# Softmax weights of a windowed attention, already with keys on the partitions: transposed after the softmax, or computed so from second scores

## The chip, the cores and the metric

One core of a Trainium2 chip runs the whole program in one launch. The metric is device time in microseconds, median of several runs. All data are float32.

## What is computed

A gated cross-attention block, then a gated mixture of expert biases, on x of shape (8, 512, 2048): 8 batches, 512 features D, 2048 positions S. Only the attention is touched by the change.

```python
x = x + tanh(g_xattn[0]) * xattn(layernorm(x, axis=-1), ctx, masks, Wq, bq, Wk, bk, Wv, bv, Wo, bo)
x = x + tanh(g_ffn[0]) * ffn(layernorm(x, axis=-1), router_weight, router_bias, expert_bias)

def xattn(qk, v, masks, ...):          # DK = 256, H = 8 heads of dh = 32, windows of W = 128 positions
    qp, vp, mp = patches of 128 positions of qk, v, masks
    q = Wq @ qp + bq;  k = Wk @ qp + bk;  val = Wv @ vp + bv
    scores = einsum('bhdi,bhdj->bhij', qh, kh) / sqrt(dh)
    scores = where(mp[:, :, None, :] > 0, scores, -1e9)
    attn = softmax(scores, axis=-1)
    o = gelu(einsum('bhij,bhdj->bhdi', attn, vh))
    return (Wo @ o + bo) * masks
```

Each window of 128 positions attends only to itself, so for each window and head the scores are a 128 x 128 square (queries i, keys j). The second product contracts over the keys, and TensorE contracts over the partitions of its operands: it wants the weights with the keys on the partitions, while the softmax's row sums and maxima are taken along the free axis, with the queries on the partitions.

## The kernel before, in words

The 128 windows are handled in 64 **groups** g of two windows (NPP = 2, 256 positions); two groups make a **chunk** of 512 positions (32 chunks, four per batch). Groups with even g are the first half of a chunk, odd ones the second. The order of instructions on every engine is written out by hand (`manual_schedule`), and every engine works through its own list in order. One iteration of the main loop (line 816, 62 groups; the last two groups are written out behind it) does parts of several groups in a software pipeline:

- scores of group g (`scores`, line 412): 16 products into four PSUM banks sc0 to sc3, one bank for each of four heads that lie on 32 partitions each; each product of float32 shows as two records on TensorE;
- the weighed values of group g-2 (`weigh`, 487), and their copy to SBUF by ScalarE (`weighed`, 504, the copy is at line 480);
- row maxima (`maxima`, 431, VectorE): 16 instructions that write min(-(score + mask bias)) per row as a column `nmx`, and the negated masked scores as `at`;
- exponentials (`exps`, 446, ScalarE), in place, with row sums;
- in the old way, the division by the sums (`divide`, 458: reciprocal on VectorE, product on GpSimd), and for group g-1 four *turns*: `turn` (468) transposes four heads on TensorE, `turned` (482) copies the result to SBUF on ScalarE;
- queries and keys of the next chunk, one half of the features per group (`queries_and_keys`, 343: seven blocks of products by a Strassen-like scheme, with VectorE and GpSimd adding between them; `between` is called in it at set places);
- values of the next chunk (`values`, 391, and `values_out`, 402, which adds the bias bv on VectorE);
- even groups: layer norm of a later chunk (`norm`, 264, ScalarE), half of the output projection (`attend`, 524, two of four), and four transposes of the result for the router (`turn_x`, 549); odd groups: GELU with its table load, `table_of_exps` (212, which loads the table of the exponential back), the router's `logits` (557), and the other half of `attend`;
- at the end of each group one step of the expert mix of an earlier batch (`mix`, 749): two products pb, and two additions on VectorE that read them.

A PSUM bank that is written again must first be read out. The projections and the mix share a pool of two banks (`ps_mm`, tag mm), transposes and weighed values another of two (`ps_tr`, tag tr); from the third group on, the values of a group go into bank sc0 (`values(c_, h_, 0, 0)`), and half of `attend` in odd groups into sc1 and sc2 once the mix runs. Loads and stores are issued on SP's queue, except for the first context and x tiles, and one last store, on ScalarE's.

Of the kernel before, what the change touches and what calls it, by code (L numbers as in the profile page):

```python
# [22 lines left out]
def flamingo_gated_kernel(  # L23
# [51 lines left out]
    ps_mm = ctx.enter_context(tc.tile_pool(name="ps_mm", bufs=2, space=PSUM))  # L75
    ctx.enter_context(tc.manual_schedule())
# [46 lines left out]
    bv_sb = const.tile([P, DK], F32, name="bv_sb")  # L123
# [4 lines left out]
    gates = const.tile([P, 2], F32, name="gates")  # L128

# [24 lines left out]
    def load_rest():  # L154
# [3 lines left out]
        nc.sync.dma_start(bv_sb, bv.partition_broadcast(P))  # L158
        with nc.allow_non_contiguous_dma(reason="short bias vectors onto partitions"):
            nc.sync.dma_start(bq_sb, bq.rearrange("(t p) -> p t", p=P))  # L160
            nc.sync.dma_start(bk_sb, bk.rearrange("(t p) -> p t", p=P))
            nc.sync.dma_start(bo_sb, bo.rearrange("(t p) -> p t", p=P))
        nc.sync.dma_start(gates[:, 0:1], g_xattn.partition_broadcast(P))
# [4 lines left out]
    def load_later_weights():  # L168
        nc.sync.dma_start(wo_sb, woT.rearrange("(t p) d -> p t d", p=P))
        nc.sync.dma_start(rw_sb, rwT.rearrange("(k p) e -> p k e", p=P))  # L170

# [171 lines left out]
    def queries_and_keys(ch, e, between):  # L343
# [6 lines left out]
        s1, s5, u2, u4 = (  # L350
            work.tile([P, CW // 2], F32, tag=t, name=f"{t}_{ch}_{e}", bufs=1)
            for t in ("s1", "s5", "u2", "u4")
        )
# [14 lines left out]
        nc.vector.tensor_tensor(u2, p6, s1, ALU.add)  # L368
        banks.append(product([P, 2, CW // 2], f"qk_{ch}_{e}_1"))
# [5 lines left out]
        between(0)  # L375
# [3 lines left out]
        u3 = work.tile([P, CW // 2], F32, tag="s1", name=f"u3_{ch}_{e}", bufs=1)  # L379
# [3 lines left out]
        between(1)  # L383
# [3 lines left out]
        nc.vector.tensor_tensor(k, k, m01s[ch], ALU.mult)  # L387
# [14 lines left out]
    def values_out(ch, h):  # L402
# [3 lines left out]
        nc.vector.tensor_tensor(vT, pv, bv_sb[:, None, :].to_broadcast([P, NPP, DK]), ALU.add)  # L406
# [3 lines left out]
    pairs = {}  # L410

    def scores(g):


        ch, h = g // NH, g % NH
        sc = [ps_sc.tile([P, NPP, NE, W], F32, tag=f"sc{r}", name=f"sc_{g}_{r}") for r in range(HR)]
        rows = [slice(r * DH, (r + 1) * DH) for r in range(HR)]
        for i in range(NPP):
            ws = slice(h * HW + i * W, h * HW + (i + 1) * W)
            for e in range(NE):  # L420
                for r in range(HR):
                    nc.tensor.matmul(  # L422
                        sc[r][:, i, e, :], qss[ch][rows[r], e, ws], kss[ch][rows[r], e, ws],
                        start=True, stop=True,
                    )
        nmx = small.tile([P, HR, NPP, NE], F32, tag="nmx", name=f"nmx_{g}")
        at = [work.tile([P, H, W], F32, tag="at", name=f"at_{g}_{i}", bufs=4) for i in range(NPP)]
        rsum = small.tile([P, NPP, H], F32, tag="rsum", name=f"rsum_{g}")
        pairs[g] = {"sc": sc, "nmx": nmx, "at": at, "rsum": rsum, "atT": {}}

    def maxima(g, qs):
# [4 lines left out]
        for q in qs:  # L436
            i = q // 2
            bias = m01s[ch][:, hf * HW + i * W : hf * HW + (i + 1) * W]
            for r in (2 * (q % 2), 2 * (q % 2) + 1):
                for e in range(NE):  # L440
                    nc.vector.tensor_tensor_reduce(  # L441
                        p["at"][i][:, e * HR + r, :], p["sc"][r][:, i, e, :], bias, -1.0, BIG,
                        ALU.add, ALU.min, p["nmx"][:, r, i, e : e + 1],
                    )

    def exps(g, q):
        p = pairs[g]
        i = q // 2
        for r in (2 * (q % 2), 2 * (q % 2) + 1):
            for e in range(NE):  # L450
                h = e * HR + r
                at = p["at"][i][:, h, :]
                nc.scalar.activation(  # L453
                    at, at, AF.Exp, bias=p["nmx"][:, r, i, e : e + 1], scale=-1.0,
                    accum_out=p["rsum"][:, i, h : h + 1],
                )

    def divide(g, i, engine=None):
        p = pairs[g]
        rs = p["rsum"][:, i, :]  # L460
        nc.vector.reciprocal(rs, rs)  # L461
        (engine or nc.gpsimd).tensor_tensor(  # L462
            p["at"][i], p["at"][i], rs[:, :, None].to_broadcast([P, H, W]), ALU.mult
        )

    os_ = {}

    def turn(g, k):
# [3 lines left out]
        if e == 0:  # L472
            p["atT"][i] = work.tile([P, H, W], F32, tag="atT", name=f"atT_{g}_{i}")
# [5 lines left out]
    def copy(engine, out_, in_):  # L479
# [748 lines left out]
```

## Time and profile before

| | us |
|---|---|
| device time, median of 3 runs | 1311.58 |
| lowest and highest run | 1311.1, 1311.7 |
| span of the profiled execution | 1309.1 |
| busy: TensorE, VectorE, ScalarE, GpSimd | 1292.1, 923.7, 872.2, 796.3 |
| L476 the turns on TensorE, 1024 x 275 ns | 150.7 (they overlap) |
| L480 their copies on ScalarE, 254 x 576 ns | 140.5 |
| L422 scores on TensorE, 2048 records x 283 ns | 75.6 (they overlap) |
| L462 divisions on GpSimd, 128 x 1908 ns | 244.2 |
| DMA: 173.40 MB, mean 132 GB/s | 40% of 16 engines on SP's queue |

The profile is one execution recorded by the hardware. A line such as `618.34 1.17 PE L422 MATMUL sc<-ks,qs ... x32` in its timeline is a merged group: start and length in us, engine, source line, operation, what is written from what is read, shapes, and how many records. PE is TensorE's products, PEld its weight loads, DVE is VectorE, ACT ScalarE, POOL GpSimd; SPq and ACTq are the instructions on SP's and ScalarE's sequencers that issue DMAs. Records of one engine overlap a little, so cost is read from start to start. A bracket at a line's end is the idle time before it and what ended it.

### The profile page before, as it was taken

The page shows a single profiled execution, that of the slowest core. Times are in us where ns is not written, and L with a number is a line of the kernel's source. Part 1 is how long each engine was busy: PE and PEld are TensorE (multiplying, and loading weights), DVE is VectorE, ACT ScalarE, POOL GpSimd, SP SyncE. Part 2 cuts the span into 40 slices and gives each one's busy share as a digit, 9 for nine tenths or more (in the row PEclk, how much of TensorE's full clock was granted, in tenths as well). Part 3 has the DMA queues.
Part 4 walks back from the last instruction along what each step waited for, and adds up shares of the span by engine and source line. Part 5 has one row for each costly group of instructions (what it writes and reads, how often), then busy time and mean ns, then how long its engine had stood idle before and what let it go on. Part 6 is the DMA issues. An engine that isn't in the chain of part 4 may idle for free.

```text
span 1309.1 us, 27778 instructions
## 1 busy us (share of the span) xinstructions
PE 1292.1 (99%) x9532; PEld 941.1 (72%) x9532; DVE 923.7 (71%) x3605; ACT 872.2 (67%) x2843; POOL 796.3 (61%) x817
## 2 busy tenths in 40 slices
PE   8999999999999999999999999999999999999997
PEld 5777777777777777777777777777777777777653
DVE  5777676777677767777677776677776776666776
ACT  2776776676675766766676766677756767657654
POOL 3655456765566755566655666656666665566645
PEclk9999999999999999999999999999999999999999
DMA  8444324344345353444443453533543423423124
GB/s 273 111 126 122 112 78 137 106 161 127 116 153 162 123 167 97 136 165 142 140 148 95 154 169 124 159 108 123 165 151 132 159 63 127 138 97 106 69 78 177
DMA packets 109725, 173.40 MB, mean 132 GB/s; under 512 B 9232, under 2 KB 43664, under 8 KB 109456
## 3 DMA queue, kind: packets, MB, share of 16 engines
q1 hardware_dynamic: 107264, 168.75, 40.0%
q10 hardware_dynamic: 2320, 2.88, 0.6%
q8 instruction: 75, 1.23, 0.4%
q14 instruction: 66, 0.54, 0.1%
HBM read 138.06 MB, written 33.55 MB: 131 GB/s over the span
## 4 chain that ended last, share of the span: by engine, by line
PE 91%; ACT 3%; DVE 3%; DMA 1%; POOL 1%; issue 0%; DVEq 0%; ACTq 0%
PE qk L360 27%; PE po L528 17%; PE pv L397 15%; PE pt L476 8%; PE sc L422 5%; PE pa L498 5%; PE pb L702 5%; PE pl L563 4%; PE px L552 4%; ACT at L453 2%; DMA xr<-in_x 1%; DVE st L547 1%; DVE st L249 1%; PE pf L327 1%; ACT atT L480 0%
## 5 line engine op out<-in xcount | busy, mean ns | idle before, releaser
L462 POOL TENSOR_TENSOR at<-at,rsum 128x1024 f32<-128x1024 f32 x128 | 244.2, 1908 | 291.1 <-DVE rsum L461 269.2
L453 ACT ACTIVATE at<-at,nmx 128x128 f32<-128x128 f32 x1024 | 396.4, 392 | 3.2 <-DVE nmx L441 3.2
L397 PE MATMUL pv<-wv_sb,cx 128*128 128x256 f32 x1024 | 237.8, 380 | 1.7 <-DMA cx<-in_ctx 1.6
L528 PE MATMUL po<-o,wo_sb 128*128 128x512 f32 x512 | 234.1, 599 | 0.4 <-ACT o L522 0.4
L441 DVE CUSTOM_DVE_ANT_0 at<-sc,m 128x128 f32<-128x128 f32 x1024 | 220.7, 286 | 7.6 <-PE sc L422 7.4
L397 PEld LDWEIGHTS pv<-wv_sb,cx 128*128 128x128 f32 x1024 | 187.5, 191 | 24.8 <-DMA cx<-in_ctx 3.2
L537 POOL TENSOR_TENSOR xr<-t,xr 128x512 f32<-128x512 f32 x124 | 161.4, 1313 | 65.8 <-DVE t L534 65.7
L453 ACT ACTIVATION_READ_ACCUMULATOR at<-at,nmx 128x1 f32 x1024 | 194.9, 190 | 0.0
L480 ACT COPY o<-pa 128x512 f32<-128x512 f32 x63 | 36.9, 585 | 230.3 <-PE pa L498 230.3
L480 ACT COPY atT<-pt 128x512 f32<-128x512 f32 x254 | 140.5, 576 | 52.9 <-PE pt L476 52.7
L528 PEld LDWEIGHTS po<-o,wo_sb 128*128 128x128 f32 x512 | 94.3, 190 | 100.6 <-issue 83.9
L476 PEld LDWEIGHTS pt<-ident,at 128*128 128x128 f32 x1024 | 121.8, 141 | 57.2 <-issue 35.5
L476 PE MATMUL pt<-ident,at 128*128 128x128 f32 x1024 | 150.7, 275 | 1.3 <-ACT atT L480 0.9
L534 DVE SCALAR_TENSOR_TENSOR t<-po,bo_sb,mk 128x512 f32<-128x512 f32 x128 | 95.7, 749 | 62.5 <-PE po L528 62.2
L480 ACT COPY x1T<-px 128x512 f32<-128x512 f32 x120 | 70.2, 585 | 96.8 <-PE px L552 96.6
L360 PE MATMUL qk<-xt,wq_sb 128*128 128x256 f32 x496 | 128.0, 380 | 1.6 <-DVE u L368 1.6
L360 PE MATMUL qk<-xn,wk_sb 128*128 128x256 f32 x496 | 127.5, 380 | 0.0
L360 PE MATMUL qk<-xn,ws 128*128 128x256 f32 x496 | 127.3, 379 | 0.0
L360 PEld LDWEIGHTS qk<-xn,ws 128*128 128x128 f32 x496 | 94.2, 190 | 12.8
L720 DVE TENSOR_TENSOR xr<-pb,xr 128x512 f32<-128x512 f32 x122 | 78.2, 685 | 29.4 <-PE pb L702 29.4
L360 PEld LDWEIGHTS qk<-xn,wk_sb 128*128 128x128 f32 x496 | 89.4, 190 | 9.7
L422 PEld LDWEIGHTS sc<-ks,qs 32*128 32x128 f32 x2048 | 63.2, 186 | 45.3 <-DVE t L534 18.2
(123 smaller groups left out, 2077.7 us busy)
## 6 DMA issues: line engine op xcount, KB each, us to landing
out_dram<-xr SPq DMA_DIRECT2D x63, 512.0 KB, 3.5
cx<-in_ctx SPq DMA_DIRECT2D x61, 512.0 KB, 5.3
raw<-in_x SPq DMA_DIRECT2D x112, 256.0 KB, 3.4
xn<-in_x SPq DMA_DIRECT2D x28, 1024.0 KB, 7.8
xr<-in_x SPq DMA_DIRECT2D x28, 1024.0 KB, 7.6
mk<-in_mask_Bx1x_ff SPq DMA_DIRECT2D x32, 256.0 KB, 5.1
xr<-in_x SPq DMA_DIRECT2D x12, 256.0 KB, 6.9
cx<-in_ctx ACTq DMA_DIRECT2D x2, 512.0 KB, 8.2
```

The source lines that it names most:

```text
L360: nc.tensor.matmul(out_, w_[:, j, es], xb[:, j, :], start=(j == 0), stop=(j == NM // 2 - 1))
L397: nc.tensor.matmul(pv[:, i, :], cx[:, m, i * W : (i + 1) * W], wv_sb[:, m, :], start=(m == 0), stop=(m == NM - 1),)
L422: nc.tensor.matmul(sc[r][:, i, e, :], qss[ch][rows[r], e, ws], kss[ch][rows[r], e, ws], start=True, stop=True,)
L441: nc.vector.tensor_tensor_reduce(p["at"][i][:, e * HR + r, :], p["sc"][r][:, i, e, :], bias, -1.0, BIG, ALU.add, ALU.min, p["nmx"][:, r, i ...
L453: nc.scalar.activation(at, at, AF.Exp, bias=p["nmx"][:, r, i, e : e + 1], scale=-1.0, accum_out=p["rsum"][:, i, h : h + 1],)
L462: (engine or nc.gpsimd).tensor_tensor(p["at"][i], p["at"][i], rs[:, :, None].to_broadcast([P, H, W]), ALU.mult)
L476: nc.tensor.transpose(pt[:, r, :], p["at"][i][:, e * HR + r, :], ident)
L480: (engine.tensor_copy if engine is nc.vector else engine.copy)(out_, in_)
L528: nc.tensor.matmul(po[:, cs], wo_sb[:, e, m * P : (m + 1) * P], os_[ch][:, e, cs], start=(e == 0), stop=(e == NE - 1),)
L534: nc.vector.scalar_tensor_tensor(t[:, cs], po[:, cs], bo_sb[:, m : m + 1], mks[ch][:, cs], ALU.add, ALU.mult)
L537: (engine or nc.gpsimd).tensor_tensor(xc, t[:, cs], xc, ALU.add)
L720: nc.vector.tensor_tensor(xc, pt, xc, ALU.add)
```

## The change

For groups 0 to 60, the weights are no longer transposed. Group g's scores, maxima and exponentials are computed as before, but only for the maxima and sums. One iteration later the scores of g-1 are multiplied a second time with queries and keys exchanged (`scores_turned`), into the same four banks, so that keys lie on the partitions. There a row's maximum lies along the free axis, so the 16 columns of negated maxima of a group (and the 16 of reciprocal sums of the group before, by `inverse_sums`) are turned on TensorE (`turn_columns`: one transpose to 32 rows of 128), copied by ScalarE, written to a scratch tensor in DRAM, and read back spread over all partitions: 1 MB of maxima (`nmB`) and four pieces of 64 KB of reciprocal sums (`rB`), all six DMAs issued on ScalarE's queue (`columns_turned`, `spread`). VectorE adds the spread maxima in four pieces between the blocks of the projections (`less_maxima`), ScalarE takes two exponentials of 128 x 1024 with the key mask as bias (`exps_turned`), and the division is done after the weighing: `weighed` multiplies by `rB` on VectorE. The last three groups keep the old way.

Moved along with it: bv is added in GELU's bias, per feature (GELU in two halves), and `values_out` is a plain copy on ScalarE; the product of keys and mask goes from VectorE to GpSimd; the scratch tiles s1, u2, u3 and u4 of the projections live in the queries' and keys' own tiles; `weighed` comes later, after `attend` or `logits`; `table_of_exps` follows GELU at once. A column per window of the key mask (`key_bias`) is made at the start.

```diff
-    def values_out(ch, h):
+    def values_out(ch, h, engine=nc.scalar):
...
-        nc.vector.tensor_tensor(vT, pv, bv_sb[:, None, :].to_broadcast([P, NPP, DK]), ALU.add)
+        copy(engine, vT, pv)
...
+    def inverse_sums(g):
+        new_columns(g + 1)
+        nc.vector.reciprocal(columns_of[g + 1][:, 1], pairs[g]["rsum"])
...
+    def turn_columns(g):
+        n = 2 * NQ if g > 0 else NQ
+        pn = ps_tr.tile([n, P], F32, tag="tr", name=f"pn_{g}")
+        nc.tensor.transpose(
+            pn, columns_of[g].rearrange("p a r e i -> p (a r e i)")[:, :n], ident
+        )
...
+    def columns_turned(g):
...
+        nc.scalar.copy(t[:n], pn)
+        d = dram.tile([2 * NQ, P], F32, tag="nrD", name=f"nrD_{g}")
+        nc.scalar.dma_start(d[:n], t[:n])
...
+    def spread(g):
+        d = rows_of_columns.pop(g)
+        if g < first_plain:
+            t = work.tile([P, NQ, W], F32, tag="nmB", name=f"nmB_{g}", bufs=1)
+            nc.scalar.dma_start(
+                t.rearrange("p c w -> p (c w)"),
+                d[:NQ].rearrange("c w -> (c w)").partition_broadcast(P),
+            )
...
+            for r in range(HR):
+                nc.scalar.dma_start(
+                    t[rows[r]].rearrange("p e i w -> p (e i w)"),
+                    d[NQ + r * n : NQ + (r + 1) * n].rearrange("c w -> (c w)").partition_broadcast(DH),
+                )
...
+    def scores_turned(g):
+        p = pairs[g]
+        p["st"] = score_banks(g, kss, qss, "st")
...
+    def less_maxima(g, r):
...
+        nc.vector.tensor_tensor(
+            p["atT"].rearrange("p i (e r) w -> p r e i w", r=HR)[:, r], p["st"][r],
+            p["nmB"][:, r * n : (r + 1) * n, :].rearrange("p (e i) w -> p e i w", e=NE), ALU.add,
+        )
+    def exps_turned(g, i):
...
+        nc.scalar.activation(at, at, AF.Exp, bias=key_bias[:, k : k + 1])
```

The order of one iteration of the main loop in the changed kernel, by function, for an even group (in an odd one `logits` stands in place of the two `attend`, and GELU and the other `attend` come in the second half):

```python
scores(g); weigh(g-2); maxima(g); exps(g, 0); exps(g, 1); attend x2; weighed(g-2)
exps(g, 2); turn_columns(g); columns_turned(g); exps(g, 3); scores_turned(g-1)
queries_and_keys(...)   # with less_maxima(g-1, 0..2) between its blocks
less_maxima(g-1, 3); inverse_sums(g)
exps_turned(g-1, 0); spread(g); exps_turned(g-1, 1)
turn_x; values; norm(first half); values_out; turn_x; norm(second half); mix
```

## The prediction

> **What bounds the kernel now.** I read the page's first two parts (busy shares, slices), then its chain, then the timelines of TensorE, VectorE and ScalarE over one pair of groups in steady state, then the issue times on ScalarE's DMA queue.
>
> ```profile
> PE 1292.1 (99%) x9532; PEld 941.1 (72%) x9532; DVE 923.7 (71%) x3605; ACT 872.2 (67%) x2843; POOL 796.3 (61%) x817
> PEclk9999999999999999999999999999999999999999
> PE 91%; ACT 3%; DVE 3%; DMA 1%; POOL 1%; issue 0%; DVEq 0%; ACTq 0%
> ```
>
> TensorE is busy all the time at full granted clock, and the chain is 91% TensorE. So each microsecond taken from TensorE is a microsecond won, if TensorE still never waits. That is the question here. TensorE's timeline across the end of an even group and the start of an odd one:
>
> ```profile
> 614.58 1.89 PE L397 MATMUL pv<-wv_sb,cx 128*128 128x256 f32 x8
> 616.31 0.60 PE L552 MATMUL px<-ident,xr 128*128 128x128 f32 x4
> 616.75 0.60 PE L476 MATMUL pt<-ident,at 128*128 128x128 f32 x4
> 617.28 1.13 PE L702 MATMUL pb<-eb_sb,wT 64*128 64x512 f32 x4
> 618.34 1.17 PE L422 MATMUL sc<-ks,qs 32*128 32x128 f32 x32
> 619.44 1.08 PE L498 MATMUL pa<-atT,vT 128*32 128x128 f32 x32
> 620.45 1.94 PE L563 MATMUL pl<-x1T,rw_sb 128*64 128x512 f32 x8
> 622.32 0.66 PE L476 MATMUL pt<-ident,at 128*128 128x128 f32 x4
> ```
>
> VectorE's at the same place: the mix's additions, then 16 maxima 0.21 us apart (two rows of them), then the router's sum.
>
> ```profile
> 618.44 1.29 DVE L720 TENSOR_TENSOR xr<-pb,xr 128x512 f32<-128x512 f32 x2 [1.01 <-PE pb L702]
> 619.64 0.28 DVE L441 CUSTOM_DVE_ANT_0 at<-sc,m 128x128 f32<-128x128 f32 x1
> ...
> 622.81 0.28 DVE L441 CUSTOM_DVE_ANT_0 at<-sc,m 128x128 f32<-128x128 f32 x1
> ...
> 623.02 0.69 DVE L581 TENSOR_TENSOR lgT<-pl,lgT 128x512 f32<-128x512 f32 x1
> ```
>
> The maxima end at 623.1, 0.8 us after TensorE has gone on to the turn at 622.32. Today nothing on TensorE needs them so early. ScalarE's queue, where the kernel starts:
>
> ```profile
> 0.72 1.02 ACTq L145 DMA_DIRECT2D cx<-in_ctx  x2
> 1.76 0.49 ACTq L102 DMA_DIRECT2D cx<-in_ctx  x1
> ...
> 5.89 0.39 ACTq L102 DMA_DIRECT2D cx<-in_ctx  x1
> ```
>
> A DMA issue holds the issuer 0.39 to 0.51 us; on SP's queue, simple ones show 0.33 to 0.56.
>
> **TensorE's work.** Two turns take 0.88 us (604.18 to 605.06), so a group's four take 1.76. The second scores repeat the first, 618.34 to 619.44, 1.10. The turn of the columns is one transpose, a quarter of 0.44, 0.11. A steady group saves 0.55. Over the program, 61 groups are turned the new way and 62 turn columns: 61 x (1.76 - 1.10) - 62 x 0.11 = 33.4 us. That is all there is to win.
>
> **VectorE.** Added per group: four additions of the spread maxima (row L720, 0.60 apart), 2.4, and the weighed product on VectorE instead of ScalarE's copy, 0.6. Gone: the values' bias (0.6), the keys' mask (0.6, now GpSimd), about 0.1 of reciprocals. Net 1.7 on 14.4 of 19.8. The additions lie where VectorE waits for the projections (gaps of 0.77, 1.35 and 0.42 at 607.93 to 612.18): the first two fit, the last two push the end of the stage by some 0.8. The banks that TensorE reuses there are free 0.5 us or more earlier than it needs them, so it does not wait.
>
> **GpSimd** loses two divisions of 1.9 and gains a 512-wide product of 1.3. Nobody comes to wait: the masked keys are due a group later, and mask_bias on VectorE waits for them about 0.4 in odd groups, where VectorE has 1 us free before the values of line 534.
>
> **ScalarE.** Gone: four copies of 0.58 and the copy of o. Added: the exponentials of the turned scores, two of 128x1024, priced by gelu's row of that size (1.06, pitch 1.0); the copy of vT, 0.55; the columns' copy, about 0.25; and six DMA issues. GELU in two halves costs 0.2 in odd groups, where ScalarE ends with 2 us to spare. An issue occupies the sequencer; whether ScalarE computes meanwhile, no row shows. Bounds: all five issues of spread lie behind the first exponential (nothing after it is delayed by it), or beside it. I take beside, because ScalarE's rows start the next instruction before the last one ends (0.31 apart, 0.39 long). I take 0.42 per issue, the mean of SP's steady rows (0.37, 0.40, 0.46, 0.46).
>
> **The DMAs.** Per group 16 KB out, 1 MB of maxima and 256 KB of sums back: 78 MB more on 173. Rows of 1 MB land in 7.8 us. A broadcast is no slower: the mask row, 256 KB, is issued at 621.53 behind a 512 KB transfer of 620.20, and by the page's medians (5.1 and 5.3 us) lands at 626.6, 1.1 after it. The maxima are wanted 13 us after issue; the sums, behind them, 9.2 us after issue against about 8.9 for 1.25 MB at that rate, and VectorE has 1.7 us of slack behind that. Nothing is charged, but it is close. SP's prefetches share a set of DMA semaphores with the new ones, and may start some us late; they have half a group of slack.
>
> **Two new waits on TensorE.**
> First, the columns' turn stands ahead of the second scores and needs all 16 maxima. In even groups TensorE reaches it 1.10 + 1.01 + 3.54 = 5.65 us after the scores begin (T, 598.53), and the maxima end at T + 4.7: no wait. In odd groups it reaches it at 622.32 - 618.34 = 3.98, and the maxima end at 4.78: a wait of 0.8. Behind it in TensorE's queue stand the second scores and the projections.
> Second, vT's copy is now ScalarE's, and it frees bank sc0, which the next scores write first. Before, VectorE did it at 616.76, in time. In an even group after the change, TensorE would start the next scores at T + 19.81 - 0.55 = T + 19.26. ScalarE cannot start the turned exponentials before the fourth addition, which follows the last projection: block 6 ends at T + 13.8, VectorE then ends at 15.05. Then exponential and issues from 15.15, 5 x 0.42, to 17.3; second exponential to 18.3; x1T copy 18.8; two norms, 2 x 0.76, to 20.3; vT copy 20.85; scores at T + 20.95. That is 1.7 late. The scores' delay covers the wait for maxima (VectorE has caught up by then), so the pair pays the larger of the two, not both. Odd groups have no norms (except seven, with time for them) and no such delay: vT is out 2 us before it is due.
>
> **Sum.** There are 30 pairs even to odd. 22 have norms there: 1.7 - 1.1 = +0.6 each, +13.2. The other 8 have none, ScalarE is 0.2 late, the maxima decide: 0.8 - 1.1 = -0.3 each, -2.4. In total +10.8 on the profiled execution's 1309.1; the runs' median 1311.6 lies 2.5 above that span (launch and end, which don't change), so **1322**.
>
> [...]
>
> **Rivals.**
> *ScalarE is not late (faster).* If issues cost little or are wholly hidden, ScalarE is 0.6 late, and the maxima's 0.8 decides all 30 pairs: 30 x -0.3 = -9, **1302.6**. The forecast turns into a gain for the 22 pairs below 0.30 per issue; the smallest row seen is 0.33. At 0.33 the sum is +0.9, no change. For it: a margin of 0.1 us per issue. Against: every row.
> *ScalarE stands still during issues (slower).* The exponential does not overlap: 1.0 more per pair, 2.7 late with norms and 1.2 without: 22 x 1.6 + 8 x 0.1 = +36, **1348**. With 0.51 per issue, 22 x 2.05 + 8 x 0.55 = +50, 1361. Overlapped at 0.56: 22 x 1.3 - 2.4 = +26, 1338.
> *No wait at all (faster).* TensorE stays full: -33.4, **1278**. It needs the 16 maxima 0.8 us earlier; VectorE's additions of the mix stand ahead of them in order, so I give it little.
> *The sums land late (slower).* From 9.2 + 1.7 = 10.9 us after issue, VectorE reaches the projections late and TensorE waits for a bank; each us beyond costs up to 1 us in 60 groups: at 12 us, +60, **1380**.
>
> **How the numbers follow.** Forecast (issues beside the exponential, 0.30 to 0.56 each) 0.45, of which 0.10 falls within 0.2% (the bound of what a measurement can tell here, 2.6 us) and 0.02 faster; ScalarE not late 0.25; ScalarE standing still 0.20; no wait 0.04; late sums 0.06. Faster 0.02 + 0.25 + 0.04 = 0.31; same 0.10; slower 0.33 + 0.20 + 0.06 = 0.59. The range takes in the first rival, 1302.6 with 2.6 for its error, and ends between the two prices of the second, 1356; the 1278 and 1380 cases and half of the dearer price stay outside. The forecast's own range is 1310 to 1338.
>
> **What would show it.** In the changed trace: no pt in groups up to 60, st at 1.10 us per group. TensorE's first sc of odd groups waiting for ScalarE's vT, about 1.7 us, 22 times; nearly no wait in even groups. Columns' turn waiting for the last maximum by 0.8 in the other pairs only. Five DMA issues on ScalarE's queue per group, 0.42 each, beginning while the exponential runs. TensorE's busy time down by 30 to 35 us. I am wrong if the wait for vT is absent, if even groups wait for the columns too, or if VectorE waits for spread data.

## The result, and the profile after

| | before | after |
|---|---|---|
| device time, median (lowest to highest), us | 1311.41 (1311.1 to 1311.7) | 1438.34 (1436.84 to 1440.19) |
| span of the profiled execution, us | 1309.1 | 1438.4 |
| mean granted TensorE clock over the span | 0.999 | 0.969 |

The ratio is 1.0969, with a 95% interval of 1.0954 to 1.0985. The forecast was 1322 with a range of 1300 to 1356. The sign was right, the size was not: 127 us lost, where 11 were forecast.

The page of the changed kernel, in the parts that were shown of the kernel before:

```profile
PE 1310.7 (91%) x10571; PEld 929.3 (65%) x10571; DVE 1065.4 (74%) x3728; ACT 906.8 (63%) x2815; POOL 639.1 (44%) x757
...
PEclk9879999999999999999999999999999999999999
...
PE 70%; DVE 9%; ACT 9%; DMA 4%; issue 3%; ACTq 2%; POOL 2%; DVEq 0%; POOLq 0%
```

TensorE is now idle for 9% of the span. Its busy time rose, though work was removed: where the granted clock is lower, in early groups above all, the same products take longer (a group's first scores took 2.09 us at 158.22, with a clock of 0.64 over 158 to 166, and 1.17 at 750.92, with 1.00 over 750 to 757). The chain hands over to VectorE and ScalarE 18% of the time, and "issue", ACTq and DMA have 9%.

What TensorE waited for, by line (sum in us, times, longest). Before, its largest entry was 1.6 us.

```profile
PE sc L430 <- ACT vT L391: 71.9, 33, 6.0
PE pn L501 <- DVE nr L463: 23.4, 23, 4.1
```

Both forecast waits are there, in the forecast places (and, in the first groups, in others too). Next, TensorE's timeline from an even group (ends with pb) into an odd one, in steady state; a bracket is the idle time before the line and its releaser:

```profile
748.06 1.13 PE L792 MATMUL pb<-eb_sb,wT 64*128 64x512 f32 x4
750.92 1.17 PE L430 MATMUL sc<-ks,qs 32*128 32x128 f32 x32 [1.73 <-ACT vT L391]
...
755.72 0.27 PE L501 MATMUL pn<-ident,nr 128*32 128x128 f32 x1 [0.75 <-DVE nr L463]
755.92 1.17 PE L430 MATMUL st<-qs,ks 32*128 32x128 f32 x32
```

The first wait is 1.73, for which the forecast had 1.7. But the same group then waits 0.75 again, where the forecast had only the larger of the two. VectorE has caught up by then, and it does not help: before its first maximum it stands idle for 1.60 us, and what releases it is the scores.

```profile
752.11 0.29 DVE L463 CUSTOM_DVE_ANT_0 at<-sc,m 128x128 f32<-128x128 f32 x1 [1.60 <-PE sc L430]
```

ScalarE's side of the same place (ACTq are the DMA issues on its sequencer):

```profile
744.98 1.15 ACT L554 ACTIVATE atT<-atT,key_bias 128x1024 f32<-128x1024 f32 x1 [1.37 <-DVE atT L546]
745.07 0.34 ACTq L521 DMA_DIRECT2D nmB<-nrD  x1
745.53 1.78 ACTq L530 DMA_DIRECT2D rB<-nrD  x4
747.36 1.15 ACT L554 ACTIVATE atT<-atT,key_bias 128x1024 f32<-128x1024 f32 x1 [1.23 <-issue]
...
750.30 0.57 ACT L391 COPY vT<-pv 128x512 f32<-128x512 f32 x1
```

The issues begin while the exponential runs, as the forecast took it; the five outlast it, and the second exponential starts 1.23 us late. An early group, at 148 us, looks different:

```profile
148.04 0.34 ACTq L521 DMA_DIRECT2D nmB<-nrD  x1
148.55 5.04 ACTq L530 DMA_DIRECT2D rB<-nrD  x4
153.65 1.15 ACT L554 ACTIVATE atT<-atT,key_bias 128x1024 f32<-128x1024 f32 x1 [4.52 <-DMA rB<-nrD]
...
157.52 0.56 ACT L391 COPY vT<-pv 128x512 f32<-128x512 f32 x1
```

The last of rB's four issues comes at 153.29, 5.25 us after nmB's; by the trace's semaphore events nmB landed at 153.27. ScalarE's next instructions stand behind it, vT's copy among them, and TensorE waits 4.98 us (158.22). ScalarE waited in this way eight times:

```profile
ACT atT L554 <- DMA rB<-nrD: 34.4, 8, 4.5
```

Where the time went is read from the start of each group's first scores, after minus before: 25.1 us late at group 4, 70.0 at group 14, 124.2 at group 62, 129.1 at group 63. So three stretches have causes of their own: groups 0 to 13 (70 us, forecast as if they were like the rest), groups 14 to 61 (54), and the end (5).

### The profile page after: what moved, and what is told of

It reads as the page before. It is cut to its first block, busy times and chain, and to the rows that moved or that the text cites. A ratio compares the mean times of both kernels' runs of the same rounds, so it can differ in the third digit from the quotient of the medians.

```text
span 1438.4 us, 30638 instructions
## 1 busy us (share of the span) xinstructions
PE 1310.7 (91%) x10571; PEld 929.3 (65%) x10571; DVE 1065.4 (74%) x3728; ACT 906.8 (63%) x2815; POOL 639.1 (44%) x757
## 4 chain that ended last, share of the span: by engine, by line
PE 70%; DVE 9%; ACT 9%; DMA 4%; issue 3%; ACTq 2%; POOL 2%; DVEq 0%; POOLq 0%
PE qk L361 26%; PE po L618 13%; PE pv L401 9%; DVE at L463 5%; PE st L430 5%; PE sc L430 5%; ACT xn L273 4%; PE pa L585 4%; PE px L642 3%; PE pb L792 2%; DMA rB<-nrD 2%; PE pl L653 2%; ACTq L530 2%; ACT vT L391 1%; POOL qs L382 1%
## 5 line engine op out<-in xcount | busy, mean ns | idle before, releaser
L474 ACT ACTIVATE at<-at,nr 128x128 f32<-128x128 f32 x1024 | 396.1, 390 | 140.8 <-DVE nr L463 116.4
L554 ACT ACTIVATE atT<-atT,key_bias 128x1024 f32<-128x1024 f32 x122 | 140.1, 1148 | 190.9 <-DVE atT L546 91.6
L376 POOL TENSOR_TENSOR ks<-qs,s 128x256 f32<-128x256 f32 x62 | 45.2, 729 | 434.9 <-DVE s L375 434.8
L401 PEld LDWEIGHTS pv<-wv_sb,cx 128*128 128x128 f32 x1024 | 192.5, 191 | 28.0 <-DMA cx<-in_ctx 2.6
L474 ACT ACTIVATION_READ_ACCUMULATOR at<-at,nr 128x1 f32 x1024 | 193.6, 189 | 0.0
L546 DVE TENSOR_TENSOR atT<-st,nmB 128x512 f32<-128x512 f32 x244 | 166.1, 681 | 0.0
L430 PE MATMUL sc<-ks,qs 32*128 32x128 f32 x2048 | 82.5, 298 | 76.8 <-ACT vT L391 71.9
L430 PEld LDWEIGHTS sc<-ks,qs 32*128 32x128 f32 x2048 | 69.2, 199 | 123.0 <-ACT vT L391 72.3
L361 PE MATMUL qk<-xn,wk_sb 128*128 128x256 f32 x496 | 137.9, 402 | 0.0
L624 DVE SCALAR_TENSOR_TENSOR t<-po,bo_sb,mk 128x512 f32<-128x512 f32 x128 | 95.5, 748 | 56.6 <-PE po L618 56.0
L361 PEld LDWEIGHTS qk<-xn,wk_sb 128*128 128x128 f32 x496 | 92.0, 196 | 18.3 <-issue 0.7
L361 PEld LDWEIGHTS qk<-xt,wq_sb 128*128 128x128 f32 x496 | 89.2, 190 | 9.4
```

Source lines behind the costliest of these rows:

```text
L361: nc.tensor.matmul(out_, w_[:, j, es], xb[:, j, :], start=(j == 0), stop=(j == NM // 2 - 1))
L401: nc.tensor.matmul(pv[:, i, :], cx[:, m, i * W : (i + 1) * W], wv_sb[:, m, :], start=(m == 0), stop=(m == NM - 1),)
L430: nc.tensor.matmul(banks[r][:, e, i, :], stationary[ch][rows[r], e, ws], moving[ch][rows[r], e, ws], start=True, stop=True,)
L474: nc.scalar.activation(at, at, AF.Exp, bias=columns_of[g][:, 0, r, e, i : i + 1], scale=-1.0, accum_out=p["rsum"][:, r, e, i : i + 1],)
L546: nc.vector.tensor_tensor(p["atT"].rearrange("p i (e r) w -> p r e i w", r=HR)[:, r], p["st"][r], p["nmB"][:, r * n : (r + 1) * n, :].rear ...
L554: nc.scalar.activation(at, at, AF.Exp, bias=key_bias[:, k : k + 1])
```

## The experiments

"Late at g14, g62, g63" is the start of that group's scores in the profiled execution, minus that of the kernel before. Before, an ordinary even group lasts 19.81 and an odd one 19.88 us. The last two columns are medians over groups 14 to 60.

| kernel | median us | ratio, 95% interval | late at g14, g62, g63 | even | odd |
|---|---|---|---|---|---|
| changed kernel | 1438.34 | 1.0954 to 1.0985 | 70.0, 124.2, 129.1 | 21.27 | 20.74 |
| e1 sums first | 1414.36 | 1.0755 to 1.0801 | 44.0, 100.0, 105.4 | 21.31 | 21.11 |
| e2 vT before norms | 1400.71 | 1.0662 to 1.0698 | 62.0, 86.4, 92.8 | 19.87 | 20.30 |
| e3 columns later | 1413.86 | 1.0760 to 1.0801 | 57.6, 93.7, 100.0 | 21.27 | 20.01 |
| e4 spread on SP | 1358.01 | 1.0328 to 1.0362 | 27.6, 41.4, 47.3 | 19.93 | 20.30 |
| e5 vT on VectorE | 1370.67 | 1.0430 to 1.0462 | 41.5, 56.6, 61.6 | 19.61 | 20.40 |
| e6 no loads | 1356.25 | 1.0325 to 1.0353 | 25.2, 39.0, 45.2 | 19.93 | 20.30 |
| e7 one rB | 1362.20 | 1.0369 to 1.0401 | 32.5, 47.0, 53.1 | 19.97 | 20.30 |
| c1 three moves | 1313.67 | 1.0010 to 1.0028 | 11.0, -2.0, 4.1 | 19.47 | 19.58 |
| c2 four moves | 1316.17 | 1.0020 to 1.0043 | 12.4, -0.5, 5.2 | 19.47 | 19.58 |
| e8 mask on VectorE | 1324.10 | 1.0078 to 1.0109 | 15.1, 8.4, 12.6 | 19.47 | 19.67 |
| c3 ends again | 1305.07 | 0.9945 to 0.9970 | 4.7, -8.3, -6.7 | 19.47 | 19.58 |
| c4 all on ScalarE | 1318.94 | 1.0039 to 1.0066 | 19.1, 6.2, 7.8 | 19.47 | 19.58 |

The theory after the result: ScalarE's queue is what TensorE waits for. Early, one of rB's issues waits for nmB to land, because of a shared completion semaphore (a counter that each of this kernel's 729 DMAs raises 16 times in the trace, the last time when it has landed): in this trace the DMAs of SP and ScalarE use the same eight, in all 721 cases where one follows another on the same semaphore its issue starts after that one's landing (by 0.015 us or more), and in eight early groups (3 and 5 to 11) rB's fourth piece gets the one that nmB took, eight DMAs before in seven of them (in the group shown, four loads on SP and three pieces stand between), six in group 11. In all eight the trace has this issue 0.02 us after nmB's landing. The expectations below say ten groups; in the trace it is eight. From group 12 on the two no longer share one. In the steady state two waits add up. The rivals: the loads themselves (their traffic, or late landing), or the lower clock.

**e1: the sums' loads ahead of the maxima's**

```diff
         d = rows_of_columns.pop(g)
-        if g < first_plain:
-            t = work.tile([P, NQ, W], F32, tag="nmB", name=f"nmB_{g}", bufs=1)
...
         if g > 0:
             t = work.tile([P, NE, NPP, W], F32, tag="rB", name=f"rB_{g - 1}", bufs=1)
...
+        if g < first_plain:
+            t = work.tile([P, NQ, W], F32, tag="nmB", name=f"nmB_{g}", bufs=1)
...
```

> The same six DMAs on ScalarE's queue, the four pieces of sums ahead of the 1 MB of maxima. Theory (shared completion slots): in ten early groups the built program gives the fourth piece of sums the completion semaphore that the maxima's transfer, eight DMAs earlier, still holds; its issue, and ScalarE behind it, stand until 1 MB has landed, 3 to 4.5 us. With the pieces first no DMA on ScalarE's queue follows a fresh large one: no issue over 1.1 us, ten groups win 3 to 4 us each and the slow clock behind their waits, 1438 becomes 1395 to 1405; groups from 14 on unchanged. Rival (the DMA queue itself is full of descriptors, or data lands late): the waits stay or move to the next group, over 1430.

Measured 1414.4, against 1395 to 1405 and at least 1430: neither range. At group 14 it is 44.0 late instead of 70.0, and later groups lose as much as before. So the order of the same five issues is worth 26 us, all of it early. The theory had priced this too high: in groups 5, 6, 7, 9 and 11 a vT wait of 1.9 to 3.0 us remains. An early group has no mix and is 0.9 us shorter (18.95 against 19.81 in the kernel before), so ScalarE has less time there.

**e2: vT's copy ahead of the norms**

```diff
+            for c_, h_ in vals:
+                values_out(c_, h_)
             if nxt < last and (nxt + 1) % NCH:
                 norm(nxt + 1, (0, 1))
-            for c_, h_ in vals:
-                values_out(c_, h_)
```

> The copy of vT on ScalarE comes ahead of the two norms (1.5 us) in even groups. Theory (the bank sc0 is what TensorE waits for): its wait of 1.73 us at the start of odd groups falls to about 0.2; the wait for the maxima, 0.75, stays, since the maxima cannot begin before the bank's last product; 22 pairs with norms win 1.5, 33 us, and early groups a little more: 1398 to 1405. Rival (as the prediction had it, the larger of the two waits counts, VectorE being late anyway): the wait for the maxima grows to 0.8 where it was hidden, gain 0.9 a pair, 1418.

Measured 1400.7, in the theory's range. In an even-to-odd transition of this kernel:

```profile
729.60 1.18 PE L430 MATMUL sc<-ks,qs 32*128 32x128 f32 x32 [0.33 <-ACT vT L391]
...
734.41 0.27 PE L501 MATMUL pn<-ident,nr 128*32 128x128 f32 x1 [0.76 <-DVE nr L463]
```

The first wait fell from 1.73 to 0.33 and the second stayed at 0.76. If the pair paid the larger of the two, the removal of the larger would have gained only the difference. The waits add.

**e3: the columns' turn after the first projection block, in odd groups and group 0**

```diff
+        def lead():
+            turn_columns(g)
+            columns_turned(g)
+            exps(g, 3)
+            if g1 is not None:
+                scores_turned(g1)
...
         p1 = block(0, w11, x_[:, d1, c1])
+        lead()
```

> In odd groups (and group 0) the columns' turn and the second scores come after the first block of projections, 0.87 us later in TensorE's order. Theory (the wait for the maxima adds to the wait for the bank): the 0.75 us at the columns' turn vanish in all odd groups, 24 late ones and some early, 20 us: 1415 to 1420. Rival (the two waits cover each other): the 0.75 comes back as a longer wait elsewhere, within 5 us of 1438.

Measured 1413.9, 1 us better than the theory's range. Odd groups last 20.01 (median) instead of 20.74; the most common value is 19.58, 0.30 below the kernel before. The wait for maxima is gone from the steady state, and the even groups keep 21.27.

**e4: the spread loads issued from SP**

```diff
-            nc.scalar.dma_start(
+            nc.sync.dma_start(
...
-                nc.scalar.dma_start(
+                nc.sync.dma_start(
```

> The five loads of spread are issued on SP's queue instead of ScalarE's; ScalarE still writes the columns out. Theory (issue time on ScalarE): five issues of 0.31 to 0.43 stand between the two exponentials, 1.2 us more than the first one covers; without them vT is 1.2 us earlier in every even group, 24 us, and the ten early groups lose their wait for the shared slot on ScalarE, 35 us: about 1380. Rival (SP's order): the loads stand in SP's queue ahead of stores and prefetches and behind their waits, so VectorE or TensorE waits for data instead: 1420 or more.

Measured 1358.0; the theory said about 1380, so the issues on ScalarE cost some 80 us, and not the 59 worked out. The early loss drops to 27.6 us, 21.9 of it in groups 0 to 3; the even groups drop to 19.93. The loads are the same and as many, so their traffic is hardly the cause; e6 tests that.

**e5: vT copied by VectorE again** (one part of the change undone)

```diff
-    def values_out(ch, h, engine=nc.scalar):
+    def values_out(ch, h, engine=nc.vector):
```

> One part undone: vT is again copied out of PSUM by VectorE, as before the change, and no longer by ScalarE; all else is the changed kernel. Theory: the wait of 1.73 us before the odd groups' scores comes from ScalarE's order (the norm of the next chunk stands ahead of the vT copy), so it goes; VectorE has idle time there, since its maxima wait for the scores. Even groups fall from 21.26 to about 19.9 us, odd ones stay at 20.3 or get up to 0.6 longer: 1395 to 1410 in all, with the 70 us of the first fourteen groups still mostly there. Rival: the loads' traffic or the fallen clock, and not ScalarE's order, is what delays the scores: 1430 or more.

Measured 1370.7, lower than the theory's 1395 to 1410. The even groups gained as it said (19.61). But the early loss fell as well, to 41.5 us: the stops of ScalarE's queue are still there, and TensorE felt them mainly through vT.

**e6: no spread loads**

```diff
+        if g == 0:
+            once["nmB"] = work.tile([P, NQ, W], F32, tag="nmB", name="nmB_once", bufs=1)
+            nc.gpsimd.memset(once["nmB"], -9.0)
...
         if g < first_plain:
...
-            nc.scalar.dma_start(
...
+            pairs[g]["nmB"] = once["nmB"]
...
+            pairs[g - 1]["rB"] = once["rB"]
```

> The spread loads are left out (nmB and rB are filled once with constants and used by all groups), so the output is not the reference's; the columns' turn, its copy and its small store stay. Theory: what the loads cost is the place of their issue on ScalarE, and neither their landing nor their traffic; taking them off ScalarE altogether should then give little more than issuing them from SyncE gave (1358.0): 1340 to 1358, with the wait at the columns' turn of 0.75 us in odd groups and the 20 us of groups 0 to 3 still there. Rival: the 160 GB/s that they move, or their late landing, slow the rest down as well: 1330 or less.

This kernel leaves the loads out and takes constants in place of the maxima and sums. Measured 1356.3, in the theory's range and within 2 us of e4. Moving 76 MB (61 x 1.25; that is 56 GB/s over e4's span, not the 160 of the expectation) or not moving it is the same, if ScalarE does not issue it. That rules out traffic and late landing as more than a small cause: without the loads groups 0 to 3 lose 17.5 us instead of 21.9.

**e7: rB in one load, still on ScalarE**

```diff
-            for r in range(HR):
-                nc.scalar.dma_start(
-                    t[rows[r]].rearrange("p e i w -> p (e i w)"),
-                    d[NQ + r * n : NQ + (r + 1) * n].rearrange("c w -> (c w)").partition_broadcast(DH),
-                )
+            s_ = d[NQ:].rearrange("(r c) w -> r (c w)", r=HR)
+            nc.scalar.dma_start(
+                t.rearrange("p e i w -> p (e i w)"),
+                s_[:, None, :].to_broadcast([HR, DH, n * W]),
+            )
```

> One edit of the changed kernel: the four pieces of rB (64 KB each) are loaded by one instruction on ScalarE, with the same bytes and after nmB as before; two issues in place of five. Theory: in the first groups the fourth piece waits because it takes the same completion semaphore as nmB, eight DMAs earlier; a single one comes fewer than eight later, so the waits of 4 to 6 us behind nmB's landing go and about 25 of the 70 us lost by group 14 with them, as with the sums first (1414). ScalarE is rid of three issues also, so that vT is copied up to 1.2 us sooner in the later groups, and the wait there falls from 1.73 to 0.5 or more: 1375 to 1405. Rival: ScalarE waits for the landing of nmB itself, or for the traffic: 1430 or more.

Measured 1362.2, better than the theory's 1375 to 1405, and far from the rival. ScalarE in steady state:

```profile
772.80 1.15 ACT L554 ACTIVATE atT<-atT,key_bias 128x1024 f32<-128x1024 f32 x1 [1.37 <-DVE atT L546]
772.86 0.33 ACTq L521 DMA_DIRECT2D nmB<-nrD  x1
773.28 0.54 ACTq L530 DMA_DIRECT2D rB<-nrD  x1
773.87 1.15 ACT L554 ACTIVATE atT<-atT,key_bias 128x1024 f32<-128x1024 f32 x1
```

Two issues fit beside the exponential, and the second follows at once, 1.07 after the first; with five it came 2.38 after. The wait for vT is 0.4. So three issues fewer, for the same bytes, are worth 76 of the 127 us: 37 by group 14 and 39 later. rB lands later in this form, not sooner (see c4), so it is the issues.

**c1: e2, e3 and e4 together**

> Three moves together: the loads issued from SyncE, the vT copy ahead of the next norm on ScalarE, and in odd groups and in group 0 the columns' turn and the second scores after the first projection block. Theory: the waits are separate terms, so that the gains add: from 1358.0 (loads on SyncE) some 0.4 us by 30 for the vT copy, 0.7 us by 31 for the columns and some 8 us in the first groups: 1312 to 1328. Rival: the waits stand behind one another, so that removing one shows the next, or the columns' rows now land too late for the additions: 1340 or more.

Measured 1313.7, in the theory's range: the gains add. Even groups are at 19.47 and odd ones at 19.58, 0.34 and 0.30 below the kernel before. That is what the change is worth where nothing waits. Left over are 12.5 us in groups 0 to 3 and 6.1 at group 62.

**c2: c1, with the ends changed**

```diff
     weigh(h0 - 2)
-    weighed(h0 - 2)
...
         attend(z - 2, m, tag=t_raw)
+    weighed(h0 - 2)
...
+        if g == 0:
+            queries_and_keys(nxt, h, between, lambda: None)
+            lead()
```

> As the three moves together, and besides at both ends: in the group of the last half chunk the weighted sums of two groups before are taken out of PSUM after the maxima and the last output products, not ahead of them, and in group 0 the columns' turn stands after all of the projections. Theory: 5 us at the end and 3 to 8 us at the start fewer than the three moves alone, 1300 to 1318, so about the kernel before. Rival: at the ends other work was late too, and nothing beyond 2 us is gained.

Measured 1316.2: the rival. Group 0 got 2.9 us shorter and group 1 waited 3.85 instead of 2.48 for its maxima. The last half chunk is as late as before, so weighed was not what it waited for. The trace of c1 names it: TensorE's scores there wait 2.22 for line 625, and VectorE's timeline has the mask ahead of that line.

```profile
1228.67 2.18 DVE L306 TENSOR_SCALAR m<-m 128x512 f32<-128x512 f32 x1
1230.77 0.19 DVE L483 RECIPROCAL rsum<-rsum 128x8 f32<-128x8 f32 x1
1230.88 2.42 DVE L638 BATCH_NORM_STATS2 st<-xr 128x6 f32<-128x512 f32 x4
1233.22 1.39 DVE L625 SCALAR_TENSOR_TENSOR t<-po,bo_sb,mk 128x512 f32<-128x512 f32 x2
```

Line 306 took 2.18 us here. In the kernel before it took 0.46 in the mean. GpSimd's division (line 485) ran beside it from 1228.65 to 1230.57, and line 306 ended 0.28 us after that.

**e8: c1, with the keys' mask back on VectorE**

```diff
-        nc.gpsimd.tensor_tensor(k, k, m01s[ch], ALU.mult)
+        nc.vector.tensor_tensor(k, k, m01s[ch], ALU.mult)
```

> The three moves together (1313.7), and the product of the keys with the mask back from GpSimd to VectorE, as before the change. Theory: with the product on GpSimd, VectorE's two operations on the mask ran beside it and took 1.11 and 1.24 us in place of 0.59 and 0.46; with it back they return to those, so that VectorE's sum hardly changes (42 more, about 38 fewer), and the time moves by less than 4 us: 1310 to 1317. The wait of 2.2 us ahead of the last half chunk's first scores, where the longer mask operation stands in front of what they wait for, becomes shorter. Rival: VectorE gains by the move as predicted, the mask operations are longer for another reason, and the time grows by 5 us or more: 1319 or more.

Measured 1324.1, on the rival's side. Half of the theory holds: line 306 is back at 0.41, but line 302 does not fall (1.11, in c1 0.99), and the product takes 0.99 on VectorE where it took 0.68 before the change (0.68 here too where GpSimd is idle, 0.91 to 1.41 beside it). VectorE's busy time grows by 29 us (1058.7 to 1087.8; the product adds 61.6, line 306 takes 26.7 less), and the time by 10. GpSimd is the better place, as the change has it.

**c3: c1, with the ends changed in another way**

```diff
-        if not even:
+        if not even and nxt < last:
             mask_bias(nxt)
...
                 sums_of_x(nxt + 1, 2)
+            else:
+                mask_bias(nxt)
...
         p6 = block(1, ws2, t_[:, 0, :, :])
+        lead(2)
...
+            if n != (2 if g < 4 else 1):
+                return
...
+                if n == 2:
+                    new_queries_and_keys(nxt)
```

The last chunk's mask operation now stands behind `attend`, `lead` stands behind the second block in groups 0 to 3, and group 2 takes the new queries' and keys' tiles only then.

> The three moves together, and besides: the mask operation of the last chunk stands behind the output products' additions, and in groups 0 to 3 the columns' turn and the second scores stand after the second projection block (in group 2 too, where the new queries' tiles are then taken after them). Theory: what is left over against the kernel before sits in the waits of 3.0, 2.5, 4.4 and 1.5 us in groups 0 to 3, with the lower clock behind them (12 us), and in the wait of 2.2 us at the last half chunk (6 us with the clock); the first becomes 4 to 8 us less, the second 4 to 6: 1299 to 1307, below the kernel before. Rival: in the first groups VectorE's maxima are late whatever stands ahead, and the additions get late in turn: 1308 or more.

Measured 1305.1, as the theory said: 0.9958 of the kernel before, interval 0.9945 to 0.9970. Behind at group 14 by 4.7 instead of 11.0, and from group 62 to 63 it loses 1.6 instead of 6.1. This is the fastest version found, and the change pays in it.

**c4: c3, with the loads on ScalarE and rB in one load**

> As the last version (1305.1), but the spread loads stay on ScalarE, with rB as one load in place of four pieces; so the loads are as in the run with one rB, and the order of the vT copy, of the columns' turn and of the ends as in the last version. Theory: where the loads are issued does not matter once they are two issues and not five, since both fit beside the exponentials: 1302 to 1309. Rival: ScalarE's 0.9 us of issues per group still make vT or the columns late somewhere, and the place is worth more than 4 us: 1310 or more.

Measured 1318.9: the rival. Groups from 14 on last exactly as in c3, so in the steady state the place does not matter, as the theory said; 14 us are lost in the first eight groups. What VectorE waited for there, in c4:

```profile
DVE o L602 <- DMA rB<-nrD: 14.8, 5, 5.6
```

In c3 the same wait is 3.1 us, once. The rB that group 2 reads is issued until 58.64 and used at 68.94, 10.3 us later; c3's four pieces are issued until 61.40 and used at 67.80. So rB as one load lands later, and late sums, a rival of the prediction, do exist: in the first groups alone, five times with this form of load and once with four pieces (in the changed kernel 3.7 us, in group 2). TensorE pays for them: it waits 7.4 us, in two places, for VectorE's line 371, which stands behind the sums (1.6 us in c3). Besides, TensorE stops for 2.82 us in the middle of group 6's second scores; the last section comes back to that.

## Why the prediction was wrong

**Right.** The place of the wait for vT, and its making: the addition of issues, norms and copies. That its size came out, 1.73 us against 1.7, is partly luck: in the group shown vT let the next scores start 21.27 us after the group's own (forecast 20.95), and TensorE was ready for them at 19.54 (forecast 19.26), two errors of 0.3 that cancel. The issues run beside the exponential: the second exponential ends 3.53 us after the first began (744.98 to 748.51), where the prediction's steps gave 15.15 to 18.3, 3.15. The wait for the maxima: 0.75 against 0.8, and 0.93 in the odd groups that have no wait for vT. Late sums did not decide, and traffic hardly mattered. But two of the prediction's own signs of being wrong did show, in the first groups alone: even groups 0 and 2 wait for the columns too (4.14 and 1.32 us), and VectorE waits once for the sums (3.7 us).

**Wrong: "the pair pays the larger of the two, not both".** The prediction said that during the scores' delay VectorE catches up. It does, but to no use: the first maximum reads bank sc0, and waits for that bank's last product, the 13th of 16. In the group shown, the scores start at 750.92, that product's record ends at 752.07 and the maxima start at 752.11; before, 618.34 and 619.64, behind the mix's additions. So the maxima start with the scores, not with VectorE's free time, and a delay of the scores moves them along: the columns' turn comes 4.80 us after the scores begin, where the forecast without any delay had 4.78. e2 shows it. Price: 0.75 in 12 of the 18 odd groups from 15 on that wait for vT; in the other six the clock fell (below), and the slower products cover the wait.

**Wrong in size: "a steady group saves 0.55".** It saves 0.30 to 0.34 (c1, where no wait is left). The columns' turn takes 0.20 from start to start (755.72 to 755.92), not a quarter of a four-fold turn, 0.11. The four turns give back 1.84 in group 32 and 1.80 in group 33. The rest is lost in neighbours of the second scores: in c1's group 32 the first projections take 1.83 instead of 1.73 from start to start and the transposes for the router 1.84 instead of 1.75, and group 33 loses 0.10 and 0.11 in its first two projection blocks. Why these get longer is not shown. An ordinary pair with norms thus pays 1.73 + 0.75 - 0.64 = 1.84 where the prediction had 0.6. Measured on the pair shown (groups 32 and 33): 21.27 + 20.29 = 41.56 against 19.80 + 19.88 = 39.68, so 1.88. The pairs without norms were booked as -0.3 each; the five of them between groups 20 and 53 lost 2.54 to 2.84, by waits of 0.93 for the maxima, 1.26 to 1.48 for wT and 0.61 to 0.91 for vT.

**Wrong, and the largest: the first 14 groups were priced like the rest.** The sum multiplied a steady pair by 30. The prediction knew that the new DMAs share semaphores with SP's, but looked only at SP: "they have half a group of slack". The one that waits is ScalarE, and behind it stand vT and TensorE. e1 and e7, which change only the order or number of the issues, take 26 and 37 of the 70 us away. Another 20 lie in groups 0 to 3 (late by 21.9 at group 4 in e4, 17.5 without loads), where TensorE has neither attend nor logits to do before the columns' turn and waits 1.3 to 4.1 us at it, for maxima by the profile except in group 1; in c3 6.2 us are left of this.

**Wrong: a wait was priced at its own length.** The prediction read full clock off the page of the kernel before, and its sum has no term for slower products behind a wait. The granted clock of the changed kernel over stretches that begin with the first scores after a wait (stretch, length, TensorE busy, clock, DMA share, GB/s):

```profile
158.00:166.00 8.00, 7.78 (x72) 0.64 0.84 237
185.00:193.00 8.00, 7.86 (x105) 0.62 0.04 13
...
708.00:716.00 8.00, 7.47 (x107) 0.79 0.68 207
...
750.00:757.00 7.00, 5.33 (x105) 1.00 0.80 258
```

The first two follow waits of 4.98 and 5.90 us, the last two waits of 1.73 each. Behind all five waits for vT of 3.7 us or more the clock was lower (0.50 to 0.66 over the next 8 us): the scores at 158 take 2.09 instead of 1.17, and about 2.5 us are lost behind the wait. Behind a wait of 1.73 it fell in some groups (708) and not in others (750), at a cost of some 0.8 us (odd groups of 21.04 to 21.12 instead of 20.29). What decides between the two is not shown.

**Not foreseen:** in the groups that turn the router's weights, pb waits for ScalarE's wT, 9.0 us in 7 groups. In e4 and e7 nothing above 1 us is left of it, so it was the issues too. At group 62, VectorE's late line 306 cost 2.2 of wait and 2.7 more behind it (3.9 in c1), most of it by the clock (0.79 over the 8 us from 1360.2 in the changed kernel): c1's scores there take 2.73 us instead of 1.17.

**VectorE and GpSimd.** The product of keys and mask was moved to GpSimd, and the prediction booked 0.6 us per group as gone. VectorE's two mask operations grew instead. Their rows (count, sum in us, mean in ns), first in the kernel before, then after; lines 303 and 299 there are 306 and 302 here:

```profile
L303 DVE TENSOR_SCALAR m<-m 128x512 f32<-128x512 f32 x32 | 14.8, 462 | 1.1
L299 DVE TENSOR_SCALAR m<-mk 128x512 f32<-128x512 f32 x32 | 19.0, 592 | 0.2 <-DMA mk<-in_mask_Bx1x_ff 0.2
...
L306 DVE TENSOR_SCALAR m<-m 128x512 f32<-128x512 f32 x32 | 39.7, 1242 | 1.5
L302 DVE TENSOR_SCALAR m<-mk 128x512 f32<-128x512 f32 x32 | 35.6, 1112 | 0.0
```

Of the 42 us moved away, 41 come back here. e8 ties line 306's part of it to the product's place: in most chunks the product now pushes GpSimd's next subtraction (line 289) into line 306. Line 302's part has the same cause with another operation, by the timelines: before and after, it starts while GpSimd adds (line 537, now 627), and ends 0.28 or 0.29 us behind the addition. Before, 0.26 us of the addition are left when it starts, after, 0.88:

```profile
605.05 0.55 DVE L299 TENSOR_SCALAR m<-mk 128x512 f32<-128x512 f32 x1
...
735.16 2.50 POOL L627 TENSOR_TENSOR xr<-t,xr 128x512 f32<-128x512 f32 x2 [0.65 <-DVE t L624]
736.77 1.17 DVE L302 TENSOR_SCALAR m<-mk 128x512 f32<-128x512 f32 x1
```

The first line is of the kernel before. No run tests what makes line 302 start earlier. The prediction called VectorE's extra work hidden, and in the steady state it is; at group 62 it ends on the path.

## What to carry to other kernels

A DMA issue cost its place in a queue here (five per group moved from ScalarE to SP: 1438.3 to 1358.0): count what stands behind it on that engine, and check which earlier transfer its completion semaphore was last used by. A wait that delayed a producer delayed all that read it (1.73 and 0.75 us in one group), so add two waits in one group unless a row shows the second being absorbed. Price the first and last iterations apart from the steady state, and before a change is given up, look which of its waits are only order: here a loss of 9.7% became a gain of 0.4% with the same arithmetic.

## What the runs showed of the hardware

- DMA instructions issued on ScalarE's sequencer while an exponential ran (745.07 within 744.98 to 746.13). In the steady state each held it 0.31 to 0.45 us, with two exceptions of 0.71 and 1.05; in the stretches shown, one load with a 256 KB target held it 0.54, and four of 64 KB held it 1.78 together.
- In the changed kernel's trace no DMA was issued before the one ahead of it on the same completion semaphore had landed (721 cases, 0.015 us after the landing at the least). In eight groups rB's fourth piece came 0.02 us after the landing of the 1 MB load that held its semaphore, some 4.9 to 5.3 us after that load's issue, and the exponential behind it on ScalarE waited too, 34.4 us in sum.
- One load of 256 KB whose source has four outer rows landed later than four loads of 64 KB: by the semaphore events it landed 8.1 us after its issue in c4 (median of 61), the last of c3's four pieces 5.7 us after the first one's issue. In the traces of e7 and c4 each of the 61 rB loads raised its semaphore five times, once 0.97 us after the issue and four times when it landed, where every other load raised it 16 times. Why it landed later is not shown.
- VectorE's mask operations took longer beside GpSimd's: line 306 at 723.57 took 1.48 us beside a GpSimd subtraction of 723.49 to 724.77, and 0.43 in the seven groups of the same kernel where nothing ran beside it. Of 54 mask operations (lines 302 and 306) that start during a GpSimd operation in the changed kernel, 53 end 0.28 or 0.29 us after it. What ties the two engines there is not shown.
- In five kernels (e1, e6, c2, e7, c4) TensorE stopped 1.2 to 3.2 us in the middle of group 6's second scores, before the same product each time, and the profile names no releaser ("issue"). In c4:

```profile
149.96 0.80 PE L432 MATMUL st<-qs,ks 32*128 32x128 f32 x4 [2.82 <-issue]
```

A queue that carries instructions (q8) moves 16 KB there. In all five kernels this transfer ends 1.3 to 1.6 us before the stop does (c4: 148.46); in the other eight kernels with second scores it ended 3.4 us or more before the same product, and none of them stopped. That TensorE waited for its instructions is the author's guess from these times; no run tests it.
